# A row LSTM with a group norm in front: one weight transfer, a partly deferred first block, and a shorter scale chain

## The chip, the cores and the metric

The kernel runs on one core of one Trainium2 chip. The metric is the device time of that core in microseconds (us); a median over runs is quoted with its lowest and highest run. All runs that enter a comparison were in the fast state. A profile is one execution; its span is some 2 us shorter than the time of the same execution.

## The reference

A group norm over x (8 images, 96 channels, 128 x 128), then a row LSTM that goes down the 128 rows of the image, then a residual sum:

```python
def step(carry, row_in):                     # one image row, all images
    h, c = carry
    ss = conv_general_dilated(h, W_ss, padding=((1, 1),)) + b_ss   # 3 taps along the row
    g5 = (ss + row_in).reshape(B, 3, 4, Oc, Wd)
    f, i, o = sigmoid(g5[:, :, 0]), sigmoid(g5[:, :, 1]), sigmoid(g5[:, :, 2])
    g = tanh(g5[:, :, 3])
    c_new = f * c + i * g
    h_new = o * tanh(c_new)
    return (h_new, c_new), h_new
# its = masked conv of _gn(x) with W_is, 32 groups;  hs = lax.scan(step, zeros, rows of its)
x = x + hs
```

The group norm needs mean and variance of a whole image before its first row can be normalised, so all of x is read once for the statistics and a second time, block by block, for the recurrence.

## The kernel before

The batch is split into two halves of four images, which take turns: a half step is one row of one half. Every four rows of a half are a block; x of a block is loaded into a tile `x` (and its first 64 channels, shifted, into `xr`), and GpSimd or ScalarE normalises it into `hx` and `xn`.

The parts that the change and the argument touch, with cuts marked:

```python
def load_weights():                          # ten transfers, issued after the sixth chunk
    nc.sync.dma_start(wt[0:C, 0, :], w_ss[:, 0])
    nc.sync.dma_start(wt[C:P, 0, :], w_is[C2:C, 0])
    # ... eight more

def inputs(s, row):                          # what a half step's matmuls read
    # ... vs = even + odd and vf = odd - even on VectorE
    diff = nc.gpsimd.tensor_sub(vd, ...)     # and vd on GpSimd

class HalfStep:
    def both(self, a):                       # passes over vs and vf
        self.mm(a, 0, 1, self.vs, start=True)
        self.mm(a, 1, 2, self.vf)
    def rest(self, a):                       # a pass over xn, then two over vd
        self.mm(a, None, 4, xi)
        self.mm(a, 0, 0, self.vd[:, 1])
        self.mm(a, 1, 3, self.vd[:, 0], stop=True)

# statistics: 48 chunks of 1 MB, bn_stats on VectorE, one bn_aggr per image
chunks = {6: load_weights, 7: make_weights, 16: lambda: load(0, 0), 38: lambda: load(1, 0)}

# after the statistics: the scale chain of the second half, then its first block
Bh.means()                                   # 10 TensorE passes
Bh.squares(nc.vector)
spin(6, wt[:, 0, 0:256])
Bh.scale(nc.vector)                          # 13 small VectorE instructions
for j in range(BH):
    normalise_shared(nc.vector if j < 2 else nc.scalar, 1, 0, j, 0, 1)   # row 0, into hx
moving[1] = inputs(1, 0)
for j in range(BH):
    normalise_own(nc.vector if j < 2 else nc.scalar, 1, 0, j, 0, 1)      # row 0, into xn
# ...
for j in range(BH):
    normalise_shared(nc.gpsimd, 1, 0, j, 1, R)                           # rows 1 to 3
for j in range(BH):
    normalise_own(nc.gpsimd, 1, 0, j, 1, R)
for s in range(NH):
    load_rows(s, 1)                          # block 1
    load(s, 1)

for row in range(NT):                        # the loop: half steps (row, s), from (0, 1) on
    for s in range(NH):
        # ... now.both, gates of prev, now.rest
        prev.output()                        # h of prev, and inputs() of prev's next row
```

Since a half step's `output` makes the inputs of the same half's next row, the vd of the first half's row 1 is queued on GpSimd in half step (0, 1), behind whatever was queued there before the loop.

## Time and profile before

The median of the six runs taken with the result is 2155.81 us (2154.95 to 2158.45).

| piece | from | to | us | what sets it |
|---|---|---|---|---|
| statistics, to the end of the last aggregation | 0 | 148.80 | 148.80 | VectorE and the transfers, both near full |
| scale chain, to the first sum vs of the second half | 148.80 | 157.08 | 8.28 | a chain of short passes and instructions |
| to the first large matmul of the loop | 157.08 | 161.47 | 4.39 | TensorE and VectorE |
| the loop, 255 half steps of 7.79 us | 161.47 | 2148.69 | 1987.22 | TensorE |

The first number of a line in the chain of waits is its start, the second its length. The way to read this kernel is to ask of each change when the first large matmul starts (161.47 us) and when the third half step's starts (177.09 us). From there on one half step follows the other every 7.79 us, so an advance that is still there at that point is there at the end. Here and below "the third half step" is (1, 1), the second half's row 1, and its start is that of its first matmul over xn.

### The profile page before, as it was taken

What the parts mean: (1) busy time and instruction counts of PE and PEld (TensorE: products, weight loads), DVE (VectorE), ACT (ScalarE), POOL (GpSimd) and SP (SyncE); (2) the same over time, 40 slices, a digit from 0 to 9 for tenths busy, and PEclk for the clock granted to TensorE, in tenths of its full rate; (3) what the DMA queues carried; (4) which work ended last, traced back from release to release, by engine and by line L of the source; (5) the groups of instructions that cost most, each with busy time, mean ns of one, the idle gap of its engine ahead of it and who ended that gap; (6) DMA issues with size and microseconds to landing.
All of it is one profiled execution on the core that took longest, in us unless ns stands there. A gap on an engine that the chain in (4) does not pass through costs nothing.

```text
span 2156.1 us, 24498 instructions
## 1 busy us (share of the span) xinstructions
PE 2014.5 (93%) x7740; PEld 1451.8 (67%) x7740; DVE 1589.4 (74%) x3296; ACT 1366.7 (63%) x2582; POOL 1026.2 (48%) x1321
## 2 busy tenths in 40 slices
PE   0049999999999999999999999999999999999998
PEld 0037777777777777777777777777777777777776
DVE  7977777777777777777777777777777777777776
ACT  0226666666666666666666666666666666666666
POOL 1006554455555545555555555555445555554552
PEclk9999999999999999999999999999999999999999
DMA  9981444433344444323444432244443334444411
GB/s 353 419 253 38 105 108 108 108 89 72 73 91 108 108 108 93 77 75 79 108 108 108 99 82 74 71 105 108 108 108 88 71 74 92 108 108 108 94 44 29
DMA packets 103151, 234.77 MB, mean 109 GB/s; under 512 B 6288, under 2 KB 8432, under 8 KB 97008
## 3 DMA queue, kind: packets, MB, share of 16 engines
q1 hardware_dynamic: 103024, 233.22, 42.7%
q8 instruction: 62, 1.02, 0.2%
q14 instruction: 65, 0.53, 0.1%
HBM read 182.86 MB, written 50.33 MB: 108 GB/s over the span
## 4 chain that ended last, share of the span: by engine, by line
PE 92%; DVE 4%; DMA 3%; SPq 0%; ACT 0%; issue 0%
PE ps L329 92%; DVE bst L489 3%; DMA xn<-in_x_dram 2%; DMA piece<-in_x_dram 1%; DMA wt<-in_w_ss_dram 1%; DMA xs<-in_x_dram 0%; SPq L482 0%; PE pst L196 0%; DVE st L493 0%; DVE g L366 0%; ACT hx L252 0%; DVE hx L254 0%; DVE c L370 0%; DVE hx L384 0%; DVE x L391 0%
## 5 line engine op out<-in xcount | busy, mean ns | idle before, releaser
L329 PEld LDWEIGHTS ps<-vd,wt 128*128 128x128 f32 x3072 | 583.7, 190 | 407.1 <-issue 367.2
L329 PE MATMUL ps<-xn,wt 128*128 128x512 f32 x1536 | 795.5, 599 | 2.3 <-issue 1.2
L329 PE MATMUL ps<-vd,wt 128*128 128x256 f32 x3072 | 788.3, 379 | 0.0
L355 ACT ACTIVATE g<-ps 32x512 f32<-32x512 f32 x768 | 453.5, 591 | 469.5 <-PE ps L329 469.4
L302 POOL TENSOR_TENSOR vd<-hx 128x512 f32<-128x512 f32 x256 | 266.0, 1039 | 988.4 <-DVE vf L301 759.4
L339 ACT ACTIVATE m<-ps,bias 128x256 f32<-128x256 f32 x768 | 358.4, 467 | 182.4 <-PE ps L329 182.2
L329 PE MATMUL ps<-vs,wt 128*128 128x256 f32 x1536 | 457.0, 379 | 1.0 <-DVE vs L300 1.0
L329 PE MATMUL ps<-vf,wt 128*128 128x256 f32 x1536 | 456.8, 379 | 0.0
L359 ACT ACTIVATE ps<-ps 96x512 f32<-96x512 f32 x768 | 442.9, 577 | 16.1
L363 DVE TENSOR_TENSOR ps<-ps,c 96x512 f32<-96x512 f32 x256 | 178.0, 695 | 372.5 <-ACT ps L359 372.5
L346 DVE TENSOR_TENSOR ps<-m,ps 128x256 f32<-128x256 f32 x768 | 329.2, 429 | 26.3
L345 DVE TENSOR_TENSOR ps<-m,ps 128x256 f32<-128x256 f32 x768 | 324.2, 422 | 15.8
L391 POOL TENSOR_TENSOR x<-x,hx 96x512 f32<-96x512 f32 x254 | 328.4, 1293 | 0.0
L329 PEld LDWEIGHTS ps<-xn,wt 128*128 128x128 f32 x1536 | 270.5, 189 | 76.3 <-DVE ps L346 32.8
L329 PEld LDWEIGHTS ps<-vs,wt 128*128 128x128 f32 x1536 | 291.7, 190 | 41.2 <-DVE vs L300 0.9
L329 PEld LDWEIGHTS ps<-vf,wt 128*128 128x128 f32 x1536 | 291.8, 190 | 39.7
L366 DVE TENSOR_TENSOR g<-ps,g 96x512 f32<-96x512 f32 x256 | 175.9, 687 | 106.9 <-ACT g L355 106.9
L254 POOL TENSOR_SCALAR hx<-x,rstd,nmr 32x512 f32<-32x512 f32 (+1 forms) x252 | 203.9, 809 | 25.0
L254 POOL TENSOR_SCALAR xn<-xr,rstd,nmr 128x512 f32<-128x512 f32 (+1 forms) x252 | 204.9, 813 | 0.1
L384 DVE TENSOR_TENSOR hx<-ps,th 96x512 f32<-96x512 f32 x256 | 173.8, 679 | 0.7 <-ACT th L374 0.7
L370 DVE TENSOR_TENSOR c<-ps,g 96x512 f32<-96x512 f32 x256 | 173.8, 679 | 0.0
L374 ACT ACTIVATE th<-c 96x512 f32<-96x512 f32 x256 | 157.9, 617 | 1.9 <-DVE c L370 1.9
(61 smaller groups left out, 439.0 us busy)
## 6 DMA issues: line engine op xcount, KB each, us to landing
xr<-in_x_dram SPq DMA_DIRECT2D x124, 512.0 KB, 9.1
x<-in_x_dram SPq DMA_DIRECT2D x64, 768.0 KB, 9.3
out_dram<-x SPq DMA_DIRECT2D x62, 768.0 KB, 5.3
piece<-in_x_dram SPq DMA_DIRECT2D x16, 1024.0 KB, 12.6
xn<-in_x_dram SPq DMA_DIRECT2D x16, 1024.0 KB, 14.2
x<-in_x_dram SPq DMA_DIRECT2D x62, 256.0 KB, 6.2
xs<-in_x_dram SPq DMA_DIRECT2D x15, 1024.0 KB, 11.8
out_dram<-x SPq DMA_DIRECT2D x2, 576.0 KB, 3.7
```

Of the source, the lines that this page charges most:

```text
L254: engine.tensor_scalar(dst, src, scale, shift, ALU.mult, ALU.add)
L302: diff = nc.gpsimd.tensor_sub(vd.rearrange("p t (b j) -> p t b j", b=BH), strided(h[:, 0, 0, :], 1, [(BH * JP - 1, 2), (JP, BH), (1, J)]), ...
L329: nc.tensor.matmul(o, wt[:, p, bass.ts(a, P)], rhs, start=start, stop=stop, skip_group_check=True)
L339: nc.scalar.activation(self.m1[a], self.ps[a][:, 0:HB], AF.Identity, bias=bias[:, a : a + 1])
L345: nc.vector.tensor_add(lo, self.m1[a], hi)
L346: nc.vector.tensor_sub(hi, self.m1[a], hi)
L355: nc.scalar.activation(self.g[a * 32 : (a + 1) * 32], self.ps[a][C:P], AF.Tanh)
L359: nc.scalar.activation(gate, gate, AF.Sigmoid)
L363: nc.vector.tensor_mul(f, f, cs[self.s].rearrange("p t b j -> p (t b j)"))
L366: nc.vector.tensor_mul(self.g, self.ps[1][0:C], self.g)
L370: nc.vector.tensor_add(c, self.ps[0][0:C], self.g)
L391: (nc.gpsimd if row + 1 < NT else nc.vector).tensor_add(xo, xo, h)
```

## The change

The intent is to shorten everything before the loop. It has four parts, with the letters that the prediction gives them:

- (a) all weights, biases and the averaging matrix packed on the host into one array and one transfer;
- (b) only half of the first half's block (two rows of four) and a quarter of the second half's (one row) are loaded before the statistics end; the rest is loaded behind the last chunk, and GpSimd normalises it then;
- (c) the last chunk in two pieces;
- (d) a shorter scale chain for the second half, with the gates of the very first half step moved into its waits.

What the prediction calls (e) is what (b) puts behind the statistics. The diff, cut to its core:

```diff
 def load_weights():
-    nc.sync.dma_start(wt[0:C, 0, :], w_ss[:, 0])
-    # ... nine more
+    nc.sync.dma_start(wl, w)
@@ loads of part of a block
-def load_rows(s, k):
+def load_rows(s, k, lo=0, hi=R):
-def load(s, k):
+def load(s, k, lo=0, hi=R, copy=True):
@@ the first sums of the chain need fewer passes
 def means(self):
-    self.mm(0, 2, self.st[:, :, 0], start=True)
+    self.mm(self.dm[:, 0, :], 2, self.st[:, :, 0], start=True)
     for i in range(2):
-        self.mm(1 + i, i, self.st[:, :, 0])
-        self.mm(3 + i, i, self.st[:, :, 1])
+        self.mm(self.pv[:, i, :], i, self.st[:, :, 1], start=i == 0)
@@ the other means now come after the squares
+    for i in range(2):
+        self.mm(self.dm[:, 1 + i, :], i, self.st[:, :, 0], stop=True)
@@ statistics
-chunks = {6: load_weights, 7: make_weights, 16: lambda: load(0, 0), 38: lambda: load(1, 0)}
+chunks = {6: load_weights, 7: make_weights,
+          16: lambda: load(0, 0, 0, 2, copy=False), 40: lambda: load(1, 0, 0, 1, copy=False)}
-for piece in range(4 if n == 0 else 1):
+pieces = {0: 4, B * QW // CH - 1: 2}.get(n, 1)
@@ after the statistics
+prev.tanh(a2)
+prev.sigmoid(a2)
 Bh.means()
+prev.forget()
 Bh.squares(nc.vector)
-spin(6, wt[:, 0, 0:256])
+spin(5, wt[0][:, 0:256])
+prev.gated()
 Bh.scale(nc.vector)
 # ... row 0: hx all on VectorE, xn all on ScalarE
-first[0].forget()
-for j in range(BH):
-    normalise_shared(nc.gpsimd, 1, 0, j, 1, R)
-for j in range(BH):
-    normalise_own(nc.gpsimd, 1, 0, j, 1, R)
-    border(nc.gpsimd, 1, 0, j, 1, R)
+prev.cell()
+prev.cell_tanh()
+for s, lo in ((1, 1), (0, 2)):
+    load_rows(s, 0, lo, R)
+    load(s, 0, lo, R)
+for s, lo in ((1, 1), (0, 2)):
+    for j in range(BH):
+        normalise_shared(nc.gpsimd, s, 0, j, lo, R)
+        normalise_own(nc.gpsimd, s, 0, j, lo, R)
+        border(nc.gpsimd, s, 0, j, lo, R)
```

In the loop, the gates of `prev` are left out of the half steps of row 0, since they have been computed. Block 1's own normalisations (`OWN1`) start one row later than those of other blocks.

More of the change, by code (lines that the diff above doesn't have):

```diff
@@ L25 @@
     x: bass.AP,
-    w_ss: bass.AP,
-    w_is: bass.AP,
-    b_ss: bass.AP,
-    b_is: bass.AP,
-    gmat: bass.AP,
+    w: bass.AP,
     out: bass.AP,
@@ L68 @@
     g_pool = ctx.enter_context(tc.tile_pool(name="gates", bufs=2))
-    wt = const.tile([P, 5, 4 * C], F32, name="wt")
-    wr = const.tile([P, 2, 4 * C], F32, name="wr")
-    bias = const.tile([P, 3], F32, name="bias")
-    bias2 = const.tile([P, 3], F32, name="bias2")
-    gm = const.tile([P, 3, P], F32, name="gm")
-    def load_weights():
-        nc.sync.dma_start(wt[0:C, 0, :], w_ss[:, 0])
-        nc.sync.dma_start(wt[C:P, 0, :], w_is[C2:C, 0])
-        nc.sync.dma_start(wr[0:C, 1, :], w_ss[:, 1])
-        nc.sync.dma_start(wr[C:P, 1, :], w_is[C2:C, 1])
-        nc.sync.dma_start(wt[0:C, 3, :], w_ss[:, 2])
-        nc.sync.dma_start(wt[0:C2, 4, :], w_is[0:C2, 0])
-        nc.sync.dma_start(wt[C2:P, 4, :], w_is[0:C2, 1])
-        nc.sync.dma_start(bias, b_ss)
-        nc.sync.dma_start(bias2, b_is)
-        nc.sync.dma_start(gm, gmat)
+    O4 = 4 * C
+    wl = const.tile([P, w.shape[1]], F32, name="wl")
+    wm = const.tile([P, 3, O4], F32, name="wm")
+    tap = [wl[:, bass.ts(i, O4)] for i in range(4)]
+    bias, bias2 = wl[:, 4 * O4 : 4 * O4 + 3], wl[:, 4 * O4 + 3 : 4 * O4 + 6]
+    gm = wl[:, 4 * O4 + 6 :].rearrange("p (i q) -> p i q", i=3)
+    wt = [tap[1], wm[:, 0, :], wm[:, 1, :], tap[2], tap[3]]
+    def load_weights():
+        nc.sync.dma_start(wl, w)
     def make_weights():
-        nc.gpsimd.memset(wt[C:P, 3, :], 0.0)
         for a in range(3):
@@ L98, in make_weights @@
                 if third < 2:
-                    nc.gpsimd.memset(wr[C:P, 1, cols], 0.0)
+                    nc.gpsimd.memset(tap[0][C:P, cols], 0.0)
                 if third < 1:
-                    nc.gpsimd.memset(wt[C:P, 4, cols], 0.0)
-        nc.gpsimd.tensor_add(wr[:, 0, :], wt[:, 0, :], wt[:, 3, :])
-        nc.gpsimd.tensor_add(wt[:, 1, :], wr[:, 0, :], wr[:, 1, :])
-        nc.gpsimd.tensor_sub(wt[:, 2, :], wr[:, 0, :], wr[:, 1, :])
-        nc.gpsimd.tensor_scalar_mul(wt[:, 1:3, :], wt[:, 1:3, :], 0.5)
+                    nc.gpsimd.memset(tap[3][C:P, cols], 0.0)
+        nc.gpsimd.tensor_add(wm[:, 2, :], tap[1], tap[2])
+        nc.gpsimd.tensor_add(wt[1], wm[:, 2, :], tap[0])
+        nc.gpsimd.tensor_sub(wt[2], wm[:, 2, :], tap[0])
+        nc.gpsimd.tensor_scalar_mul(wm[:, 0:2, :], wm[:, 0:2, :], 0.5)
         nc.gpsimd.tensor_add(bias, bias, bias2)
@@ L131, with rows_of @@
     xt = {}
-    def rows_of(s, k, lo, hi):
-        return x[s * BH : (s + 1) * BH, lo:hi, k * R : (k + 1) * R, :].rearrange(
+    def rows_of(s, k, c0, c1, lo=0, hi=R):
+        return x[s * BH : (s + 1) * BH, c0:c1, k * R + lo : k * R + hi, :].rearrange(
             "b c r w -> c b (r w)"
         )
-    def load_rows(s, k):
-        nc.sync.dma_start(xr[s][0:C2, :, 1:], rows_of(s, k, 0, C2))
-        nc.sync.dma_start(xr[s][C2:P, :, 0 : R * W], rows_of(s, k, 0, C2))
-    def load(s, k):
-        t = x_pool.tile([P, BH, R, W], F32, tag=f"x{s}", name=f"x{s}_{k}")
-        flat = t.rearrange("c b r w -> c b (r w)")
-        if k > 0:
-            nc.sync.dma_start(flat[C:P], rows_of(s, k, C2, C))
-        nc.sync.dma_start(flat[0:C], rows_of(s, k, 0, C))
-        xt[s, k] = t
+    def load_rows(s, k, lo=0, hi=R):
+        src = rows_of(s, k, 0, C2, lo, hi)
+        nc.sync.dma_start(xr[s][0:C2, :, 1 + lo * W : 1 + hi * W], src)
+        nc.sync.dma_start(xr[s][C2:P, :, lo * W : hi * W], src)
+    def load(s, k, lo=0, hi=R, copy=True):
+        if lo == 0:
+            xt[s, k] = x_pool.tile([P, BH, R, W], F32, tag=f"x{s}", name=f"x{s}_{k}")
+        flat = xt[s, k].rearrange("c b r w -> c b (r w)")[:, :, lo * W : hi * W]
+        if copy:
+            nc.sync.dma_start(flat[C:P], rows_of(s, k, C2, C, lo, hi))
+        nc.sync.dma_start(flat[0:C], rows_of(s, k, 0, C, lo, hi))
     E = mybir.EngineType
@@ L164, in spin @@
                 bank[:, 0 : rhs.shape[1]],
-                wt[:, 0, 0:P],
+                wt[0][:, 0:P],
                 rhs,
@@ L170, in spin, with first_rows @@
             )
-    def first_rows(s):
-        t = xt[s, 0].rearrange("c b r w -> c b (r w)")
+    def first_rows(s, hi):
+        t = xt[s, 0].rearrange("c b r w -> c b (r w)")[:, :, 0 : hi * W]
         nc.scalar.activation(t[C:P], t[C2:C], AF.Identity)
-        nc.scalar.activation(xr[s][0:C2, :, 1:], t[0:C2], AF.Identity)
-        nc.scalar.activation(xr[s][C2:P, :, 0 : R * W], t[0:C2], AF.Identity)
+        nc.scalar.activation(xr[s][0:C2, :, 1 : 1 + hi * W], t[0:C2], AF.Identity)
+        nc.scalar.activation(xr[s][C2:P, :, 0 : hi * W], t[0:C2], AF.Identity)
     st = [const.tile([P, BH, 2], F32, tag=f"st{s}", name=f"st{s}") for s in range(NH)]
@@ L188, in __init__ @@
             self.st, self.rstd, self.nmr = st[s], rstd[s], nmr[s]
-            self.ps = ps_st.tile([P, 5, BH], F32, tag=f"st{s}", name=f"pst{s}")
+            self.dm = ps_st.tile([P, 3, BH], F32, tag="dm", name=f"dm{s}")
+            self.pv = ps_st.tile([P, 2, BH], F32, tag="pv", name=f"pv{s}")
+            self.pm = self.dm[:, 1:3, :]
             self.q = const.tile([P, BH], F32, tag=f"q{s}", name=f"q{s}")
@@ L192, in __init__ @@
             self.v = const.tile([P, 2, BH], F32, tag=f"v{s}", name=f"v{s}")
-            self.sums = self.ps[:, 1:5, :]
         def mm(self, o, i, rhs, start=False, stop=False):
-            nc.tensor.matmul(
-                self.ps[:, o, :], gm[:, i, :], rhs, start=start, stop=stop, skip_group_check=True
-            )
+            nc.tensor.matmul(o, gm[:, i, :], rhs, start=start, stop=stop, skip_group_check=True)
         def means(self):
-            self.mm(0, 2, self.st[:, :, 0], start=True)
+            self.mm(self.dm[:, 0, :], 2, self.st[:, :, 0], start=True)
             for i in range(2):
-                self.mm(1 + i, i, self.st[:, :, 0])
-                self.mm(3 + i, i, self.st[:, :, 1])
+                self.mm(self.pv[:, i, :], i, self.st[:, :, 1], start=i == 0)
         def squares(self, engine):
             if engine is nc.scalar:
-                engine.activation(self.q, self.ps[:, 0, :], AF.Square)
+                engine.activation(self.q, self.dm[:, 0, :], AF.Square)
             else:
-                engine.tensor_copy(self.q, self.ps[:, 0, :])
-                engine.tensor_mul(self.q, self.q, self.ps[:, 0, :])
+                engine.tensor_copy(self.q, self.dm[:, 0, :])
+                engine.tensor_mul(self.q, self.q, self.dm[:, 0, :])
             for i in range(2):
-                self.mm(3 + i, i, self.q, stop=True)
+                self.mm(self.pv[:, i, :], i, self.q, stop=True)
+            for i in range(2):
+                self.mm(self.dm[:, 1 + i, :], i, self.st[:, :, 0], stop=True)
         def to_sbuf(self):
-            copy = const.tile([P, 4, BH], F32, name="sums")
-            nc.scalar.activation(copy, self.sums, AF.Identity)
-            self.sums = copy
+            copy = const.tile([P, 2, 2, BH], F32, name="sums")
+            nc.scalar.activation(copy[:, 0], self.pm, AF.Identity)
+            nc.scalar.activation(copy[:, 1], self.pv, AF.Identity)
+            self.pm, self.pv = copy[:, 0], copy[:, 1]
         def scale(self, engine):
-            pm, pv = self.sums[:, 0:2, :], self.sums[:, 2:4, :]
+            pm, pv = self.pm, self.pv
             y, v, t = self.rstd, self.v, self.t
@@ L329, in mm @@
             nc.tensor.matmul(
-                o, wt[:, p, bass.ts(a, P)], rhs, start=start, stop=stop, skip_group_check=True
+                o, wt[p][:, bass.ts(a, P)], rhs, start=start, stop=stop, skip_group_check=True
             )
@@ L401 @@
     OWN, SHARED = ((0, 1), (2,), (), (3,)), ((), (0, 1), (2, 3), ())
+    OWN1, SHARED1 = ((), (0, 1), (2,), (3,)), SHARED
     def prepare(s, row):
         k, r = row // R + 1, row % R
+        own, shared = (OWN1, SHARED1) if k == 1 else (OWN, SHARED)
         if k < NB:
-            for j in OWN[r]:
+            for j in own[r]:
                 normalise_own(nc.gpsimd, s, k, j, 0, R)
                 border(nc.gpsimd, s, k, j, 0, R)
-            for j in SHARED[r]:
+            for j in shared[r]:
                 normalise_shared(nc.gpsimd, s, k, j, 0, R)
@@ L434 @@
     a0, a1, a2 = order
-    A, Bh = Scale(0), Scale(1)
+    A = Scale(0)
     moving, first = [None, None], []
     def first_block():
+        first_rows(0, 2)
         for j in range(BH):
-            normalise_shared(nc.scalar, 0, 0, j, 0, R)
-            normalise_own(nc.scalar, 0, 0, j, 0, R)
-            border(nc.gpsimd, 0, 0, j, 0, R)
+            normalise_shared(nc.scalar, 0, 0, j, 0, 2)
+            normalise_own(nc.scalar, 0, 0, j, 0, 2)
+            border(nc.gpsimd, 0, 0, j, 0, 2)
     def begin():
@@ L462 @@
         at(4, 0) + 8: lambda: (A.squares(nc.scalar), A.to_sbuf()),
-        at(4, 0) + 16: lambda: (A.scale(nc.gpsimd), first_rows(0), first_block()),
-        at(6, 12): lambda: first_rows(1),
+        at(4, 0) + 16: lambda: (A.scale(nc.gpsimd), first_block()),
+        at(6, 18): lambda: first_rows(1, 1),
         at(7, 0): lambda: spin(10, stats[6].rearrange("c n s -> c (n s)")),
@@ L470 @@
     }
-    chunks = {6: load_weights, 7: make_weights, 16: lambda: load(0, 0), 38: lambda: load(1, 0)}
+    chunks = {
+        6: load_weights,
+        7: make_weights,
+        16: lambda: load(0, 0, 0, 2, copy=False),
+        40: lambda: load(1, 0, 0, 1, copy=False),
+    }
     stats = []
@@ L479 @@
             xc = ring[n % len(ring)]
-            for piece in range(4 if n == 0 else 1):
-                size = CH // 4 if n == 0 else CH
+            pieces = {0: 4, B * QW // CH - 1: 2}.get(n, 1)
+            for piece in range(pieces):
+                size = CH // pieces
                 nc.sync.dma_start(
@@ L493 @@
         nc.vector.bn_aggr(st[b // BH][:, b % BH, :], bst.rearrange("c n s -> c (n s)"))
+    prev = first[0]
+    prev.tanh(a2)
+    prev.sigmoid(a2)
+    Bh = Scale(1)
     Bh.means()
+    prev.forget()
     Bh.squares(nc.vector)
-    spin(6, wt[:, 0, 0:256])
+    spin(5, wt[0][:, 0:256])
+    prev.gated()
     Bh.scale(nc.vector)
     for j in range(BH):
-        normalise_shared(nc.vector if j < 2 else nc.scalar, 1, 0, j, 0, 1)
+        normalise_shared(nc.vector, 1, 0, j, 0, 1)
     moving[1] = inputs(1, 0)
     for j in range(BH):
-        normalise_own(nc.vector if j < 2 else nc.scalar, 1, 0, j, 0, 1)
+        normalise_own(nc.scalar, 1, 0, j, 0, 1)
     nc.vector.memset(xn[1][0][0:C2, 0, 0, :, 0:1], 0.0)
-    first[0].forget()
-    for j in range(BH):
-        normalise_shared(nc.gpsimd, 1, 0, j, 1, R)
-    for j in range(BH):
-        normalise_own(nc.gpsimd, 1, 0, j, 1, R)
-        border(nc.gpsimd, 1, 0, j, 1, R)
+    prev.cell()
[8 more added lines that the diff above has]
+            border(nc.gpsimd, s, 0, j, lo, R)
     for s in range(NH):
@@ L514 @@
         load(s, 1)
-    prev = first[0]
     for row in range(NT):
@@ L521 @@
                 continue
+            head = row == 0
             now = HalfStep(s, row, moving[s])
             now.both(a0)
-            prev.tanh(a2)
-            prev.gated()
+            if not head:
+                prev.tanh(a2)
+                prev.gated()
             now.copy(a0)
             now.sums(a0)
-            prev.sigmoid(a2)
+            if not head:
+                prev.sigmoid(a2)
             now.both(a1)
             now.copy(a1)
-            prev.cell()
+            if not head:
+                prev.cell()
             now.sums(a1)
@@ L535 @@
             now.sums(a2)
-            prev.cell_tanh()
+            if not head:
+                prev.cell_tanh()
             prev.output()
@@ L572, in columns @@
     def columns(b):
-        return np.ascontiguousarray(np.asarray(b)[perm].reshape(3, 128).T)
+        return np.asarray(b)[perm].reshape(3, 128).T
+    w_ss = np.asarray(L0_conv_W_ss)[perm].transpose(2, 1, 0)
+    w_is = np.asarray(L0_conv_W_is)[perm, :, 0].transpose(2, 1, 0)
     group = np.arange(C) // (C // GROUPS)
@@ L580 @@
     mean[:, 2] = np.eye(128, dtype=np.float32) - mean[:, 2]
-    arrays = {
-        "x": x,
-        "w_ss": np.ascontiguousarray(np.asarray(L0_conv_W_ss)[perm].transpose(1, 2, 0)),
-        "w_is": np.ascontiguousarray(
-            np.asarray(L0_conv_W_is)[perm, :, 0, :2].transpose(1, 2, 0)
-        ),
-        "b_ss": columns(L0_conv_b_ss),
-        "b_is": columns(L0_conv_b_is),
-        "gmat": mean,
-    }
+    blocks = [
+        np.concatenate([w_ss[1], w_is[1, 64:96]]),
+        np.concatenate([w_ss[0], w_is[0, 64:96]]),
+        np.concatenate([w_ss[2], np.zeros_like(w_is[0, 64:96])]),
+        np.concatenate([w_is[0, 0:64], w_is[1, 0:64]]),
+        columns(L0_conv_b_ss),
+        columns(L0_conv_b_is),
+        mean.reshape(128, -1),
+    ]
+    arrays = {"x": x, "w": np.ascontiguousarray(np.concatenate(blocks, axis=1), dtype=np.float32)}
     nc = bacc.Bacc("TRN2", target_bir_lowering=False, num_devices=1)
```

## The prediction

> **What bounds the kernel now.** I read the page first, then the chain that ended last, then the waits of VectorE before 150 us, then the stretches of the transfers and the timeline between the two phases.
>
> The page and the chain in order of time (start, us, what):
>
> ```profile
> span 2156.1 us, 24498 instructions
> PE 92%; DVE 4%; DMA 3%; SPq 0%; ACT 0%; issue 0%
> ...
> 148.80 0.04 issue
> 148.84 2.31 PE pst L196 x10
> ...
> 152.64 0.18 DVE v L224
> ...
> 161.47 1987.22 PE ps L329 x7638
> ```
>
> The kernel has two phases. From 161.47 us to 2148.69 us TensorE runs the row steps without a gap that counts; 255 half steps make 7.79 us each. The change touches none of that loop's work. So everything is decided before 161.47 us, and at the few half steps after it, where another engine could still keep TensorE waiting. The time before has three pieces: the statistics until 148.80, the scale chain until VectorE starts the first sum of the second half (157.08), and 4.39 us until the first large matmul.
>
> What VectorE waits for while it computes statistics (us in total, times, longest):
>
> ```profile
> DVE bst L489 <- DMA xs<-in_x_dram: 12.6, 7, 3.7
> DVE bst L489 <- DMA xn<-in_x_dram: 5.0, 3, 2.8
> DVE bst L489 <- DMA piece<-in_x_dram: 4.7, 2, 2.9
> ```
>
> That is 22.3 us of 148.8. A chunk of 1 MB takes VectorE 2.47 us and lands every 2.48 us, so both are near full and only disturbances show. The waits sit at 7.45 us in the first chunks, 4.0 around the weights (0.77 and 3.25), 4.7 at the first block of the first half (1.86 and 2.83), 4.45 at that of the second (1.60 and 2.85), and 1.7 at the end. Stretches (us; then busy time and count of TensorE, its weight loads, VectorE, ScalarE, GpSimd; clock, DMA share, GB/s):
>
> ```profile
> 48.00:53.00 5.00, 0.00 (x0) 0.00 (x0) 3.13 (x7) 0.00 (x0) 0.00 (x0) 1.00 1.06 272
> 60.00:100.00 40.00, 3.31 (x14) 3.14 (x14) 39.85 (x69) 12.81 (x13) 3.49 (x19) 1.00 1.01 421
> 107.00:115.00 8.00, 0.00 (x0) 0.00 (x0) 6.37 (x11) 0.00 (x0) 0.00 (x0) 1.00 1.05 248
> 138.00:150.00 12.00, 6.33 (x23) 3.84 (x21) 9.31 (x17) 3.61 (x5) 0.00 (x0) 0.82 1.03 184
> ```
>
> The share stays full while the rate falls from 421 to 184 to 272 GB/s: there the 2 KB rows of the blocks are moved. Finally the timeline after the chain:
>
> ```profile
> 159.13 3.05 POOL L254 TENSOR_SCALAR hx<-x,rstd,nmr 32x384 f32<-32x384 f32 x4
> 162.28 0.69 POOL L254 TENSOR_SCALAR xn<-xr,rstd,nmr 128x384 f32<-128x384 f32 x1
> 165.88 1.04 POOL L302 TENSOR_TENSOR vd<-hx 128x512 f32<-128x512 f32 x1
> 170.19 1.03 PE L329 MATMUL ps<-vd,wt 128*128 128x256 f32 x4
> ```
>
> GpSimd first normalises the rest of the second half's block (159.13 to 165.88), then makes vd of row 1, which TensorE uses only at 170.19. It has 3.3 us to spare there.
>
> **What the Trainium skill says.** "DMA: Bandwidth & Descriptors", section "Rules for kernel authors": coalesce many small transfers into one. The trace agrees: the ten weight transfers are issued between 5.86 and 22.23 us, because from the third on the queue mostly waits for an older transfer to land before it issues, and the seventh chunk stands behind them, issued only at 22.35. The same page, "Latency and other measured facts", has copies slowing to about half for rows a large power of two apart; its smallest pitch is 512 KiB, ours is 64 KiB[...]. No page states what rows of 1 KB or 512 B at this pitch cost. "TensorE: Matmul & The Clock Gate", Part 1: an idle TensorE falls to half clock and needs a full busy window of about 3.4 us to return. The trace agrees: granted clock 0.61 from 152.4 to 157 us, with passes of 128x256 at 0.38 us (4.57 / 12) against 0.215 at full clock.
>
> **The change, part by part.**
>
> (a) One transfer for the weights. 986 KB at 421 GB/s are 2.35 us. The sixth chunk lands near 20.6, then weights and the seventh chunk: 20.6 + 2.35 + 2.48 = 25.4 against 27.38 now. Estimate: 2.1 us off VectorE's waits, allowing 0.1 for the disturbed sixth chunk. The removed memset of GpSimd and its shorter weight work lie beside the transfers and give nothing.
>
> (b) Half of the first half's block and a quarter of the second's are loaded before the end of the statistics. Today two chunks and 768 KB take 57.64 - 48.01 = 9.63 us, 4.66 more than two chunks; in the second half 118.04 - 107.36 = 10.68, 5.7 more. The number of rows stays at 384, only their length falls to 1 KB and 512 B. Whether such a row costs by bytes or by count no view tells; I choose a third by count, two thirds by bytes: 4.66 x (1/3 + 1/3) = 3.1, and 5.7 x (1/3 + 1/6) = 2.85. VectorE's aggregation once per image (0.81) lets transfers run ahead by some 0.7 at the first place and 1.4 at the second (chunk landed 107.36, used 108.74), so the waits become 2.4 and 1.45 in place of 4.7 and 4.45: 2.3 + 3.0 = 5.3 us off.
>
> (c) The last chunk in two pieces: VectorE can start at 144.1, when it is done with the one before, instead of 145.47; about 1.3 us off. Sum of (a) to (c): 8.7 us, statistics end at 140.1.
>
> (d) The scale chain. Ten passes (2.31 us) before the first VectorE copy become two; the gates fill VectorE's wait. From the end of the aggregation: gate 0.70, copy and product 0.4, but TensorE has six passes of 0.22 first, until 1.37, then four more to 2.4; the first scale instruction starts at 2.43 against 3.84. Twelve steps of 0.2 and one of 0.18 follow as before, four normalisations on VectorE at 0.365 take 1.5 (two and two ScalarE ones took 1.83). The first sum starts at 6.56 instead of 8.28: 1.72 us off, at 146.66. Gates and cell moved out of the first half step bring the first large matmul from 4.39 to about 3.55 after it: 0.85 off.
>
> (e) What is added behind. In the built program (not run) GpSimd's order is: vd of the second half, four normalisations of 384 columns for each of hx and xn, four each of 256 columns, and only then vd of row 1. The second set is new: by 0.69 and 0.70 at 384 and 0.81 at 512, 256 columns take 0.57, with border memsets (0.10) and hand-overs 5.5 us for the set and 6.5 for the first, 12.0 together. Worse, the transfers of the second half's rows 1 to 3 into xr wait in the built program for the last ScalarE normalisation of row 0, which reads another part of the same tile, and the copy of the upper channels stands behind them in the queue. That normalisation ends near 147.0 (145.1 + four of 0.45). In the trace the same pair of transfers, issued at 165.75 and 166.40, landed 5.2 and 7.0 us later, 7.6 after the first issue; with rows of 1.5 KB I take 6.7, and 0.9 for the copy. So GpSimd starts at 147.05 + 7.6 = 154.7, ends at 166.7, and vd of row 1 is there at 167.75. TensorE gets to it at 146.66 + 3.55 + 8.72 (170.19 - 161.47) - 0.05 = 158.9. It waits 8.8 us. Against 170.19 the pass is 2.4 us earlier. After such a pause the clock is at half: one to two windows of 3.4 us, at 0.381 for 0.215 a loss of 1.5 to 3 us; I take 2.0.
>
> Sum: 2.4 - 2.0 = 0.4 us off the median of 2155.63: 2155.2. The loop after it is TensorE's and recovers nothing.
>
> **The rivals.** The first: GpSimd's wait is hidden. Then all savings count, 8.7 + 1.72 + 0.85 = 11.3, and 2144.3 follows. For it speaks that GpSimd is busy 48% only; against it that its queue is in order, and that vd stands last in it. The second: short rows cost by count. Then (b) gives 0.7 + 0.1 instead of 5.3, the reload takes a us longer, and the kernel comes to about 2161. For it: at full share the rate halves with rows of a quarter of a chunk's packet. The third: rows cost by bytes alone. Then (b) gives about 7.5, the pause shrinks with faster reloads, and 2152 follows. The fourth: the late loads of block 1, which now wait for GpSimd's first set, starve a later step. Their first need is some 12 us after issue, and a pair lands in 7.6: little.
>
> **Range and chances.** The gain in (b) may be 0.8 to 7.5, the end of GpSimd's row 1.5 us either way, the clock 1.5 to 3. That makes 2150 to 2161, around 2155.2. Two per cent are 43 us, more than a quarter of everything before the loop: faster 0.01, within 0.98, slower 0.01.
>
> **What would show it.** VectorE's waits in the statistics near 14 us in place of 22.3, the weights leaving at most 1.7; the aggregation ending near 140; GpSimd idle some 7 us on a transfer before its first 384-column normalisation; a gap of about 9 us on TensorE before the vd pass of row 1, and granted clock 0.5 after it. If TensorE has no gap there, (e) is wrong and 2144 is right; if the waits at the two loads stay near 9 us, rows cost by count.

## The result, and the profile after

The changed kernel takes 2156.39 us, median of six runs (2155.15 to 2158.75), against 2155.81 before: the same. A ratio here is the mean time of one kernel's fast runs over that of the other's of the same rounds, so not quite the ratio of the medians: 1.0001, with a 95% interval of 0.9989 to 1.0014.

The page's span and its shares of the chain:

```profile
span 2156.0 us, 24509 instructions
PE 92%; DVE 4%; DMA 3%; POOL 1%; issue 0%; ACT 0%; SPq 0%; POOLq 0%; DVEq 0%
```

The span is the same to 0.1 us, but GpSimd (POOL) has come into the chain with 1%, where it had no share before. Next VectorE's waits for transfers in the statistics (us in total, times, longest):

```profile
DVE bst L491 <- DMA xs<-in_x_dram: 9.3, 5, 3.5
DVE bst L491 <- DMA xn<-in_x_dram: 2.7, 2, 1.9
DVE bst L491 <- DMA piece<-in_x_dram: 1.4, 2, 0.7
```

They sum to 13.4 us against 22.3. So the early part of the change works. Then the chain that ended last, from the last aggregation to the loop:

```profile
138.32 0.82 DVE st L495
...
144.26 1.69 ACT xn L244 x4
145.97 0.60 SPq L129
...
147.32 5.61 DMA x<-in_x_dram
153.12 0.69 POOL hx L246
...
166.18 1.05 POOL vd L294
167.27 1981.30 PE ps L321 x7606
```

The chain doesn't go from the scale chain into TensorE any more. It leaves it at ScalarE's normalisation of row 0, goes to the queue that issues the reload (SPq), to the reload, through GpSimd's normalisations and its vd, and only then to TensorE at 167.27 us. Before, TensorE carries the chain from 161.47. The timeline of GpSimd alone shows the same stretch with the waits in brackets:

```profile
146.64 1.04 POOL L294 TENSOR_TENSOR vd<-hx 128x512 f32<-128x512 f32 x1 [20.29 <-DVE vf L293]
153.12 0.69 POOL L246 TENSOR_SCALAR hx<-x,rstd,nmr 32x384 f32<-32x384 f32 x1 [5.44 <-DMA x<-in_x_dram]
...
161.07 0.56 POOL L246 TENSOR_SCALAR xn<-xr,rstd,nmr 128x256 f32<-128x256 f32 x1
...
166.18 1.04 POOL L294 TENSOR_TENSOR vd<-hx 128x512 f32<-128x512 f32 x1
```

GpSimd idles 5.44 us for the reload, works 13 us through both halves' rest, and the vd that TensorE needs comes last. TensorE's own timeline there:

```profile
167.27 2.07 PE L321 MATMUL ps<-vd,wl 128*128 128x256 f32 x4 [9.12 <-POOL vd L294]
169.13 1.92 PE L321 MATMUL ps<-xn,wl 128*128 128x512 f32 x2
...
173.51 1.03 PE L321 MATMUL ps<-vd,wl 128*128 128x256 f32 x4
```

It waits 9.12 us, and then four passes over vd take 2.07 us where four such passes take 1.03 at 173.51. The stretches show why (columns as in the prediction; the granted clock is the third from the end):

```profile
158.00:168.00 10.00, 0.88 (x3) 0.64 (x3) 2.47 (x6) 0.29 (x1) 8.72 (x19) 0.73 0.27 66
167.00:173.00 6.00, 5.73 (x11) 3.82 (x12) 0.00 (x0) 1.38 (x3) 3.71 (x4) 0.52 0.97 208
```

TensorE is busy 0.88 of 10 us in the first stretch, and in the second it is busy at half clock.

The balance follows from the starts of the first xn matmul of a half step. Two of these lines before and two after, from TensorE's timelines:

```profile
161.47 1.10 PE L329 MATMUL ps<-xn,wt 128*128 128x512 f32 x2 [1.05 <-DVE ps L346]
...
177.09 1.05 PE L329 MATMUL ps<-xn,wt 128*128 128x512 f32 x2
```

```profile
149.27 1.10 PE L321 MATMUL ps<-xn,wl 128*128 128x512 f32 x2
...
176.96 1.05 PE L321 MATMUL ps<-xn,wl 128*128 128x512 f32 x2
```

| half step | before | after | difference |
|---|---|---|---|
| (0, 1), the first in the loop | 161.47 | 149.27 | -12.20 |
| (1, 0) | 169.30 | 157.10 | -12.20 |
| (1, 1), the third | 177.09 | 176.96 | -0.13 |
| the last one | 2143.32 | 2143.19 | -0.13 |

The kernel is 12.2 us ahead when the loop begins and loses 12.07 of it within one half step. From the first pass over vd to the third half step 6.90 us pass before (170.19 to 177.09) and 9.69 after (167.27 to 176.96): 2.8 us go to the half clock, and the other 9.3 to the gap, in which TensorE's wait is 9.1.

### The profile page after: what moved, and what is told of

It reads as the page before. It is cut to its first block, busy times and chain, and to the rows that moved or that the text cites. A ratio compares the mean times of both kernels' runs of the same rounds, so it can differ in the third digit from the quotient of the medians.

```text
span 2156.0 us, 24509 instructions
## 1 busy us (share of the span) xinstructions
PE 2016.6 (94%) x7738; PEld 1453.0 (67%) x7738; DVE 1588.2 (74%) x3296; ACT 1359.6 (63%) x2583; POOL 1030.3 (48%) x1332
## 4 chain that ended last, share of the span: by engine, by line
PE 92%; DVE 4%; DMA 3%; POOL 1%; issue 0%; ACT 0%; SPq 0%; POOLq 0%; DVEq 0%
PE ps L321 92%; DVE bst L491 4%; DMA xn<-in_x_dram 1%; DMA xs<-in_x_dram 1%; DMA x<-in_x_dram 0%; POOL hx L246 0%; POOL xn L246 0%; DVE st L495 0%; PE pv L188 0%; ACT xn L244 0%; DVE ps L338 0%; SPq L484 0%; POOL vd L294 0%; DVE ps L337 0%; POOL xn L261 0%
## 5 line engine op out<-in xcount | busy, mean ns | idle before, releaser
L321 PEld LDWEIGHTS ps<-vd,wl 128*128 128x128 f32 x3072 | 584.7, 190 | 417.4 <-issue 367.2
L321 PE MATMUL ps<-vd,wl 128*128 128x256 f32 x3072 | 790.3, 380 | 9.1 <-POOL vd L294 9.1
L321 PE MATMUL ps<-xn,wl 128*128 128x512 f32 x1536 | 796.5, 600 | 1.4 <-DVE ps L338 1.3
L331 ACT ACTIVATE m<-ps,wl 128x256 f32<-128x256 f32 x768 | 358.8, 467 | 180.3 <-PE ps L321 180.1
L321 PE MATMUL ps<-vs,wm 128*128 128x256 f32 x1536 | 456.9, 379 | 0.1
L321 PE MATMUL ps<-vf,wm 128*128 128x256 f32 x1536 | 456.8, 379 | 0.0
L321 PEld LDWEIGHTS ps<-xn,wl 128*128 128x128 f32 x1536 | 271.1, 190 | 75.6 <-DVE ps L338 32.7
L321 PEld LDWEIGHTS ps<-vs,wm 128*128 128x128 f32 x1536 | 291.7, 190 | 40.0 <-DVE vs L292 0.5
L321 PEld LDWEIGHTS ps<-vf,wm 128*128 128x128 f32 x1536 | 291.8, 190 | 39.7
L246 POOL TENSOR_SCALAR xn<-xr,rstd,nmr 128x512 f32<-128x512 f32 (+2 forms) x256 | 206.5, 807 | 0.8
```

The costliest lines, as they stand in the source:

```text
L246: engine.tensor_scalar(dst, src, scale, shift, ALU.mult, ALU.add)
L321: nc.tensor.matmul(o, wt[p][:, bass.ts(a, P)], rhs, start=start, stop=stop, skip_group_check=True)
L331: nc.scalar.activation(self.m1[a], self.ps[a][:, 0:HB], AF.Identity, bias=bias[:, a : a + 1])
```

## The experiments

Eight kernels ran, each in five rounds with the kernel before on the same chip. Two calls of four: e1 to e4 on one chip (there before: 2158.09 us, median of 35 runs, 2153.73 to 2163.74), and e5 and b1 to b3 on another (there before: 2158.63, median of 32). The second call had two runs far outside, one of before at 2474 us and one of b2 at 4627 us, which aren't counted as fast and enter no ratio. All results were correct. e1 to e5 start from the changed kernel, b1 to b3 from the kernel before. Differences in us are the ratio less one times the 2158 us of before. An earlier build of e4, which the record doesn't hold, read a border that nothing had written; it never ran on a chip and was mended before e4 ran.

The theory: the savings before the loop are real, and what takes them back is only that the vd of row 1 stands last in GpSimd's queue, behind a reload that starts late. The rivals: the reload and the short rows are themselves at fault, or the savings were not worth what the prediction says.

### e1: the vd of row 1 first

```diff
-for s, lo in ((1, 1), (0, 2)):
+def rest_of_block(s, lo):
     # four shared normalisations, then four own ones with borders, then block 1's loads
@@ in the loop, behind prev.output()
+            if (row, s) == (0, 1):
+                rest_of_block(1, 1)
+            if (row, s) == (1, 0):
+                rest_of_block(0, 2)
```

> The changed kernel, but GpSimd makes vd of row 1 before it normalises the rest of the first block (rest of the second half after the first half step, rest of the first half after the next). Theory (GpSimd's order holds up TensorE by 9.1 us and the half clock after it costs some 3 more): no gap of TensorE before the vd pass of row 1, no half clock near 165 us, 12 us less than the changed kernel, so about 2144.4 us. Rival (the gain of the statistics is lost elsewhere, for instance in the loop with its weights in another tile): about 2156 as now.

Measured: 2146.79 us (2144.17 to 2147.46), ratio 0.9946 (0.9934 to 0.9958), 11.7 us faster than before. GpSimd's timeline at the vd of row 1:

```profile
152.88 1.04 POOL L294 TENSOR_TENSOR vd<-hx 128x512 f32<-128x512 f32 x1 [4.58 <-DVE vf L293]
```

And rows of the waits of all engines from 135 to 200 us:

```profile
POOL xn L246 <- DMA xr<-in_x_dram: 5.5, 1, 5.5
...
PE ps L321 <- POOL vd L294: 0.7, 1, 0.7
```

The vd is ready at 153.9, so TensorE doesn't stop there (between 156 and 173 us it is busy throughout, at clock 1.00): the third half step starts at 165.52 and is 15.64 us behind the first one, as before (15.62), where the changed kernel takes 27.69. All of the work that the change added is still done, in the same amount, but behind the vd. One small cost appears: block 1's loads are now issued later, GpSimd waits 5.5 us for them, and one half step takes 8.78 us in place of 7.79.

### e2: whole blocks loaded early again

```diff
-16: lambda: load(0, 0, 0, 2, copy=False),
-40: lambda: load(1, 0, 0, 1, copy=False),
+16: lambda: load(0, 0, copy=False),
+38: lambda: load(1, 0, copy=False),
@@ first rows over all four rows again; no reload; GpSimd normalises rows 1 to 3
@@ of the second half only
```

> The changed kernel with its second part undone: both first blocks are loaded whole before the end of the statistics (chunks 16 and 38), so GpSimd has only the second half's rows 1 to 3 and waits for no transfer. Theory: VectorE's waits at the two loads return from about 4.1 to about 9.2 us, statistics end 5 us later than in the changed kernel, the gap and the half clock (12 us) go: about 2149.4 us. Rival (the deferred loads are a gain, and what costs is something else): slower than the changed kernel by 5 us, about 2161.

Measured: 2152.56 us, median of 14 (2148.07 to 2156.88), ratio 0.997 (0.996 to 0.9981), 6.5 us faster than before. So the deferring as the change does it costs more than it saves; without (b) the other three parts give 6.5 us. A caution: the profiled run of this kernel, at 2155.29, is one of its slower ones, and its first large matmul starts at 158.84, only 2.6 us earlier than in the profile before. VectorE's waits for transfers scatter by some us from run to run, so the size is taken from the 14 runs, not from this profile.

### e3: TensorE kept busy through the gap

```diff
+            if (row, s) == (1, 0):
+                for _ in range(19):
+                    nc.tensor.matmul(Bh.full[:, 0:64, :], wt[0][:, 0:P], ..., start=True, stop=True)
                 now.rest(a0)
```

Nineteen passes of 128x256 over weights, into a bank that nobody reads, stand in the gap.

> The changed kernel with 19 matrix products of 128x256 into a bank that nobody reads, standing before the pass of TensorE that waits for vd of row 1; they fill about 8.2 of its 9.1 us gap. Theory: vd comes at the same time as before, the clock stays full, and only the loss from the half clock goes: 2.5 to 3 us less, about 2153.6 us. Rival (the clock after the pause costs nothing): 2156.4 as now.

Measured: 2155.0 us, median of 19 (2153.09 to 2156.24), ratio 0.9985 (0.9979 to 0.9992), 3.2 us faster than before. TensorE's timeline behind the gap:

```profile
166.42 1.13 PE L322 MATMUL ps<-vd,wl 128*128 128x256 f32 x4 [1.37 <-POOL vd L295]
```

The four passes over vd take 1.13 us in place of 2.07: the clock stayed at 1.00. From the first to the third half step 25.43 us pass in place of 27.69, 2.26 less; but in this profile the vd also comes 0.43 us later after the first half step. Counted from the first vd pass to the third half step, 7.00 us pass in place of 9.69, so the half clock costs 2.7 us by the profiles; by the times, against the changed kernel's 1.0001, it is 0.16% or 3.5 us.

### e4: the reload freed from its wait

Row 0 of the second half is copied into tiles of its own, so the reload of rows 1 to 3 doesn't touch a tile that ScalarE still reads.

```diff
+fs = const.tile([P, BH, W], F32, name="fs")
+fr = const.tile([P, BH, W + 1], F32, name="fr")
-at(6, 18): lambda: first_rows(1, 1),
+at(6, 18): first_row_apart,              # ScalarE copies row 0 into fs and fr
@@ the row-0 normalisations of the second half
-    normalise_shared(nc.vector, 1, 0, j, 0, 1)
+    norm(nc.vector, ..., fs[C:P, j, :], ...)
-    normalise_own(nc.scalar, 1, 0, j, 0, 1)
+    norm(nc.scalar, ..., fr[:, j, 0:W], ...)
```

> The changed kernel with row 0 of the second half in tiles of its own, so that the reload of rows 1 to 3 waits for no normalisation of row 0 and goes out behind the last chunk. Theory: GpSimd starts its 384-column normalisations right after its first vd, near 148 instead of 153.1 us; its order is unchanged, so a gap of about 4 us stays on TensorE and perhaps half clock after it: 5 to 7.5 us less, 2149 to 2151.5 us. Rival (the wait for the reload is hidden, only the order counts): 2156 as now. Rival (the reload beside the last chunk delays the statistics): their end moves from 139.1 to some us later and eats the gain.

Measured: 2151.89 us (2151.22 to 2152.61), ratio 0.9973 (0.9962 to 0.9983), 5.8 us faster than before. TensorE's wait for the vd of row 1:

```profile
PE ps L332 <- POOL vd L305: 4.0, 1, 4.0
```

It is 4.0 us in place of 9.1, and GpSimd's first normalisation of 384 columns starts at 146.00, right behind the vd of the second half, with no wait for a transfer. So 5.1 of the 9.1 us of the gap were the reload's late issue, and the other 4.0 are GpSimd's own 13 us of work standing ahead of the vd. The second rival has fallen too: the last aggregation ends at 137.34, not later than the changed kernel's 139.12.

### b1: the single weight transfer alone, on the kernel before

```diff
-    nc.sync.dma_start(wt[0:C, 0, :], w_ss[:, 0])
-    # ... nine more
+    nc.sync.dma_start(wl, w)
@@ the weights packed on the host; make_weights and the matmuls read wl and wm
```

> The kernel before with its weights in one transfer, nothing else. Theory: the seventh chunk lands 2.2 us earlier (25.2 for 27.4 us) and all that follows keeps that: about 2.1 us less than the kernel before. Rival (the gain is given back at the first block's load, where transfers and VectorE meet again): within 0.5 us of before.

Measured: 2153.82 us, median of 20 (2150.72 to 2160.69), ratio 0.9981 (0.9973 to 0.9989), 4.1 us faster than before, with an interval of 2.4 to 5.8. VectorE's timeline at the seventh chunk, first of the kernel before and then of b1:

```profile
20.84 2.47 DVE L489 BATCH_NORM_STATS2 bst<-xn 128x6 f32<-128x512 f32 x4 [0.77 <-DMA xn<-in_x_dram]
...
27.40 4.97 DVE L489 BATCH_NORM_STATS2 bst<-xs 128x6 f32<-128x512 f32 x8 [3.25 <-DMA xs<-in_x_dram]
```

```profile
24.25 4.96 DVE L478 BATCH_NORM_STATS2 bst<-xs 128x6 f32<-128x512 f32 x8 [1.52 <-DMA xs<-in_x_dram]
```

The wait at the seventh chunk falls from 3.25 to 1.52 and the 0.77 before the sixth is gone. That makes 2.5 us: from the start of the fifth chunk to that of the seventh 9.80 us pass before and 7.31 in b1, and 7.30 in the changed kernel. The seventh chunk is used 3.15 us earlier in all; the other 0.65 comes from the first chunks, which were ready earlier in this execution. The edit doesn't touch them, as the weights are issued after the sixth, and the changed kernel's profile doesn't show it. The first large matmul starts at 158.60, 2.9 us earlier. The expected 2.1 lies somewhat below the 2.5, and just below the interval by time.

### b2: the shorter chain and the moved gates alone, on the kernel before

```diff
-Bh.means()
+prev.tanh(a2)
+prev.sigmoid(a2)
+Bh.means()                # two passes ahead of the first copy, not ten
+prev.forget()
 Bh.squares(nc.vector)
-spin(6, ...)
+spin(5, ...)
+prev.gated()
 Bh.scale(nc.vector)
@@ no gates of prev in the half steps of row 0
```

> The kernel before with the shorter scale chain and the first half's gates in its waits, nothing else. Theory: first sum of the second half 1.7 us earlier after the aggregation, first large matmul another 0.85 us earlier, no gap on TensorE because GpSimd had 3.3 us to spare: about 2.6 us less than before. Rival (GpSimd then ends too late): a wait of TensorE for vd of row 1 and less than 1 us gained.

Measured: 2155.85 us, median of 13 (one run of 4627 us left out of the ratio), ratio 0.9993 (0.9985 to 1.0002), 1.5 us faster than before with an interval of 3.2 faster to 0.4 slower. By the time this is inconclusive: it fits the expected 2.6, and nothing at all as well. The profile settles the length of the chain but not the sum. From the end of the last aggregation to the first large matmul it takes 10.15 us, against 12.67 in the profile before: 2.5 shorter. The same profile lost that earlier, by a transfer that came late among the last chunks:

```profile
149.69 2.47 DVE L491 BATCH_NORM_STATS2 bst<-xn 128x6 f32<-128x512 f32 x4 [3.05 <-DMA xn<-in_x_dram]
```

No part of the edit is near those transfers; I take it for the scatter that e2 shows too, but no run here shows its cause.

### b3: the deferred rows alone, on the kernel before

```diff
-chunks = {..., 16: lambda: load(0, 0), 38: lambda: load(1, 0)}
+chunks = {..., 16: lambda: load(0, 0, 0, 2, copy=False), 40: lambda: load(1, 0, 0, 1, copy=False)}
@@ behind the row-0 normalisations, as in the changed kernel
+for s, lo in ((1, 1), (0, 2)):
+    load_rows(s, 0, lo, R)
+    load(s, 0, lo, R)
+# ... and both sets of normalisations on GpSimd, ahead of the loop
```

> The kernel before with the deferred rows of the first blocks alone. Theory: statistics end about 5 us earlier, but the reload waits for the last normalisation of row 0, here on VectorE, 2 us after the first sum; GpSimd makes vd of row 1 near 175 us against 166.9, TensorE waits some 13 us in front of it and runs at half clock after it: about 8 us more than before. Rival (the deferral itself is a gain and the loss in the changed kernel comes from how its parts meet): 2 to 5 us less than before.

Measured: 2165.9 us (2164.87 to 2167.09), ratio 1.0038 (1.0025 to 1.005), 8.2 us slower than before. The waits behind the statistics:

```profile
PE ps L330 <- POOL vd L303: 10.5, 1, 10.5
...
POOL hx L255 <- DMA x<-in_x_dram: 7.6, 1, 7.6
```

The first large matmul starts at 156.88, 4.6 us earlier, which is what the shorter loads save, and then TensorE stands still for 10.5 us and runs on at half clock. This is the changed kernel's loss with only one of its gains. The rival, in which the deferring gains by itself, has fallen.

### e5: e1 with block 1's own normalisations a row later

```diff
-OWN1, SHARED1 = ((), (0, 1), (2,), (3,)), SHARED
+OWN1, SHARED1 = ((), (), (0, 1), (2, 3)), SHARED
@@ and e1's edit
```

> As e1_vd_first, with the second block's first two own normalisations a row later, because in that run GpSimd waited 5.5 us for their transfer and TensorE 0.7 us for the vd behind them. Theory: that wait goes and a little clock or slack with it: about 1 us less than e1_vd_first, so 12.5 us less than the kernel before. Rival (the 0.7 us are made up elsewhere): the same as e1_vd_first, 11.5 us less.

Measured: 2145.41 us (2144.57 to 2146.51), ratio 0.9944 (0.9931 to 0.9957), 12.1 us faster than before. All that TensorE still waits for the other engines' inputs of a half step, from 135 to 200 us:

```profile
PE ps L321 <- DVE vs L292: 0.2, 1, 0.2
```

The 8.78 us half step of e1 is 7.79 again, and no wait of GpSimd for a transfer is left. The times of e1 and e5 lie too close (0.9946 and 0.9944) to tell them apart; the profile is what shows the removed us. e5 is the fastest version measured, ahead of both kernels by some 0.56%.

## Why the prediction was right

The predicted time was 2155.2 us, with no difference beyond 2%; 2156.39 us came. (The 2155.63 that it starts from is the median of the runs known then; the six give 2155.81.) More than that, the mechanism was the one predicted: large savings up to the loop, given back in one wait of TensorE for the vd of row 1 and the half clock behind it. That the sum came within 0.3 us in the profiles is partly luck: the loop began 0.9 us earlier than predicted (149.27 for 150.21), and the gap and the clock together cost 1.1 to 1.3 us more. By its own steps:

| step of the prediction | predicted | profile after |
|---|---|---|
| VectorE's waits in the statistics | 14 | 13.4 |
| seventh chunk used | 25.4 | 25.24 |
| waits at the first half's block | 2.4 | 2.66 (0.73 + 1.93) |
| waits at the second half's block | 1.45 | 1.40 (0.63 + 0.77) |
| aggregation ends | 140.1 | 139.12 |
| first scale instruction after it | 2.43 | 2.46 |
| first sum vs after it | 6.56 | 6.68 |
| first large matmul after that sum | 3.55 | 3.47 |
| reload, first issue to landing | 7.6 | 6.96 (145.97 to 152.93) |
| GpSimd's two sets | 12.0 | 13.0 (153.12 to 166.17) |
| vd of row 1 ready | 167.75 | 167.22 |
| TensorE's gap | 8.8 | 9.1 |
| half clock | 2.0 | 2.8 (from the first vd pass to the third half step) |
| sum, against before | -0.4 | -0.13 |

**(a), (c) and the statistics.** The aggregation ends 9.68 us earlier (148.80 to 139.12) where 8.7 was said. Of that, 8.9 are waits of VectorE, and 0.7 is work of VectorE that no longer stands there (125.89 us busy up to 148.80 before, 125.20 up to 139.12 after). The term of (a) was too small: 2.5 us by the profiles of b1 and of the changed kernel (4.1 by b1's time, interval 2.4 to 5.8) in place of 2.1, because the whole wait of 0.77 before the sixth chunk went, where 0.1 had been allowed; at the seventh 1.73 went, where 2.0 had been said. One reading there was inexact: the queue of weight transfers waits from the fourth on, not from the third, which is issued at 6.93 without a wait. Part (c) did not run alone. In the changed kernel VectorE has no wait at the last chunk, which is what it was to bring. But (c) without (b) still has 1.3 us of waits there (e2), and (b) without (c) 1.6 (b3), against 1.4 before; its share of the time is not shown.

**(b), the rows.** The choice of a third by count and two thirds by bytes held only for the longer rows. From landing to landing, two chunks and the load take 8.06 us in the first half (45.07 to 53.13), so rows of 1 KB cost 8.06 less two chunks of 2.48, 3.1: the predicted figure. In the second half 6.63 us (108.59 to 115.22) leave 1.67 for rows of 512 B, where 2.85 was predicted. By bytes alone it would be a quarter of 5.7, 1.43. That the wait there still came out as predicted (1.40 for 1.45) is luck: the transfers ran ahead by only 0.27 (1.67 less 1.40), where 1.4 had been allowed, and the two errors cancel. The prediction also overlooked a section that bears on this. "DMA: Bandwidth & Descriptors", "Why small descriptors are slow (HBM only)", has a fixed overhead of about 3 cycles a packet beside 32-byte beats. With a row taken as one packet, an estimate from this page is 19 cycles for 512 B, 35 for 1 KB and 67 for 2 KB. That makes 5.7 x 19 / 67 = 1.6, close to the measured 1.67, and for 1 KB 4.66 x 35 / 67 = 2.4, below the measured 3.1. It hardly differs from bytes alone (1.4 and 2.3), so these two figures don't test the overhead; and 3 cycles of 67 would not bring the rate from 421 to 184 to 272 GB/s. Why the rows of a block are slow stays open: no run separates their length from their pitch. The rival "short rows cost by count" has fallen.

**(d), the chain.** Every step of it is within 0.12 us of the profile. b2's chain is 2.5 us shorter in its own profile, as said (1.72 + 0.85), though b2's time alone would not have shown it.

**(e), the gap.** e1 shows that the whole of it hangs on the order on GpSimd: with the vd first, and all the added work kept, the third half step is 15.64 us behind the first again and the kernel is 11.7 us faster than before. e4 splits the gap: 5.1 us come from the late reload, 4.0 from GpSimd's work. The wait that the prediction read out of the built program, a transfer into xr held back by ScalarE's read of another part of that tile, is in the chain above: the transfer is issued at 145.97, as the last of the four normalisations from 144.26 ends, and without that tie (e4) between 118.82 and 124.13. Two terms were too small and one too large: GpSimd's sets took 13.0 in place of 12.0, the clock 2.8 in place of 2.0, the reload 0.6 less than said. "TensorE: Matmul & The Clock Gate", "Part 1: The HAM clock gate (the "warmup" mystery)", puts the return at one busy window or more, of about 3.4 us each, on a free-running grid. In the three profiles with such a gap the half clock lasts 5.5 us after TensorE resumes (167.27 to 172.7), 5.6 in b3 (176.28 to 181.8) and 5.4 in e4 (160.73 to 166.1): about 1.6 windows each time, inside the "one to two windows" of the prediction, which a free-running grid allows. The cost of 2.8 us lies near the upper end of its 1.5 to 3.

**The rivals.** "GpSimd's wait is hidden", 2144.3, was false for this kernel, but it is the right size for the repaired one: e5 takes 2145.41. "Rows by bytes alone", 2152, came near for rows of 512 B (1.43 for 1.67), not for those of 1 KB (2.33 for 3.1), and was wrong about the time, because the pause did not shrink (9.1 us, where 8.8 had been predicted). "The late loads of block 1 starve a later step" cost nothing in the changed kernel; in e1, where they come later still, it is real and costs 1.0 us.

The parts that ran alone sum to -4.1 - 1.5 + 8.2 = +2.6 us, with (c) missing, for which 1.3 us were predicted; the whole is at +0.2. Each term has an interval of about 2 to 3 us either way, so the sums agree within what was measured. Only (b) has a sign that depends on the others: 8.2 us slower alone and 6.7 slower on top of the other three (e2 against the changed kernel), but a gain once the vd goes first. e1 is 5.2 us faster than e2, both on the same chip (2158 x (0.997 - 0.9946)), which fits (b) at last paying the prediction's 5.3 us, with about 3 us either way.

## What to carry to other kernels

Work that is put off joins an in-order queue at its new place: look at what stands behind it there, and put first what the bounding engine needs first. A dozen us won before a steady loop can be lost in a single wait of the loop's engine, and the time alone then says "no effect"; two starts, at the loop's entry and a few steps in, show both halves. A transfer into part of a tile may wait for a reader of another part, so rows that are reloaded apart belong in tiles apart.

## What the Trainium skill lacked or had wrong

- "DMA: Bandwidth & Descriptors", "Latency and other measured facts": its row pitches start at 512 KiB. While rows of 2 KB at a pitch of 64 KiB are moved, the rate is 184 to 272 GB/s at a full DMA share, against 421 with chunks alone. No page has what shorter rows cost there: 384 rows cost 4.66 and 5.7 us at 2 KB, 3.1 at 1 KB and 1.67 at 512 B. No run here separates the pitch from the length of the rows.
- "TensorE: Matmul & The Clock Gate", "Part 1: The HAM clock gate (the "warmup" mystery)": it speaks of at least one busy window of about 3.4 us. Here 5.4 to 5.6 us passed at half clock after each of three pauses of 4.0 to 10.5 us; for planning, about 1.6 windows fit these three better than one.
- "GPSIMD Engine Reference", "3.1 Elementwise — side-by-side cycle accounting": it has rates per element, a measured loop of 512 elements (769 ns at 1.8 cycles each) and a measured sum of two tensors, but no length-independent part for a scale and shift. By that rate alone 256 columns would be 0.38 us (an estimate). Here a scale and shift takes 0.57, 0.69 and 0.81 us at 256, 384 and 512 columns, so about 0.33 us fixed and 0.94 ns a column, and some 0.1 us passes between instructions; with eight border memsets of 0.10 and one instruction that took 0.98 in place of 0.57, that makes the 13.0 us.
- No page says that a transfer into one part of a tile can be held back, in the built program, by a read of another part. Here it cost 5.1 of the 9.1 us (4.0 left in e4).
